# Two graph layers on one core: graphs singly in a pipeline, with x^T of layer 0 by DMA on 16-bit halves

## The chip, the cores and the metric

The kernel runs on one core of one Trainium2 chip. The metric is the device time of one execution in microseconds (us). The kernel before takes 3158.67 us, the median of three runs (3156.97 to 3158.88). The profiled execution spans 3156.3 us, with a mean granted TensorE clock of 0.996.

Engines are named as in the profile: PE is the matrix engine (PEld its weight loads), DVE the vector engine, ACT the scalar engine, POOL the general engine that also issues the accumulating DMAs, and SP the engine that issues plain DMAs. Each engine works through its own instructions in the order of the program and waits where a result of another engine is missing.

## What is computed

32 graphs of 512 nodes with 256 features, fp32 throughout. Each graph passes two layers with 8 heads of 32 features each; the layers have different masks, and only the first has a feed-forward part. Cut to what matters:

```python
# layer 0; allowed = (adj > 0) | (adj^T > 0) | eye
q, k, v = split(x @ Wqkv.T + bqkv)                     # 8 heads of 32
attn = softmax(where(allowed, q k^T / sqrt(32), -inf))
x1 = layernorm(x + (attn v) @ Wo.T + bo) * g1 + b1
ff = relu(x1 @ W1.T + b1) @ W2.T + b2                  # 256 -> 1024 -> 256
x2 = layernorm(x + layernorm(x1 + ff) * g2 + b2)
# layer 1; mask = adj != 0, other weights
out = layernorm(x2 + (softmax(mask(q k^T / sqrt(32))) v) @ Wo1.T + bo1)
```

The graphs do not depend on each other, so work of different graphs can be interleaved at will.

## The kernel before

A `Graph` object has one method for each step. The methods that matter here (p tiles are 128 x 2048 fp32, four heads by 512 queries, for one of the four blocks of 128 keys; k = 0 to 7 counts four key blocks for each of two head groups):

```python
def transpose(self, src, h):              # x^T on PE, half h of the nodes
    if h == 0:
        self.tile("xT", [ND, N], bufs=1)
    ps = ps_d.tile([P, ND, 2 * P], F32, tag="d", ...)
    for c in range(ND):
        for j in range(2):
            nc.tensor.transpose(ps[:, c, j*P:(j+1)*P], src[:, 2*h+j, c*P:(c+1)*P], ident)
    nc.scalar.copy(self.xT[:, :, h*2*P:(h+1)*2*P], ps)
...
def scores(self, layer, k):               # 4 heads at once, 32 rows of the array each
    s = ps_s.tile([P, HPC, N], F32, tag="s", ...)       # one buffer (bufs=1)
    for j in range(HPC):
        nc.tensor.matmul(s[:, j, :], self.kT[...], self.qT[...], start=True, stop=True)
    p = work.tile([P, HPC, N], F32, tag="p", ..., bufs=8)
    nc.scalar.activation(p, s, AF.Exp, scale=SCALE)
def masked(self, layer, k):
    nc.vector.tensor_tensor(p, p, m[:, k % NQ, None, :].to_broadcast(...), ALU.mult)
def product(self, k): ...                 # psA += v^T p, 4 heads; after kc 3 ACT copies it to cT
def pair(self, k):                        # p[k] += p[k+1] by an accumulating DMA from POOL
    nc.gpsimd.dma_start(out=self.p[k], in_=self.p[k + 1], accum_op=ALU.add)
def fold(self, dst, a, b):                # p[dst] = p[a] + p[b] on DVE
    nc.vector.tensor_tensor(self.p[dst], self.p[a], self.p[b], ALU.add)
def sums(self, k, hg, first, last):       # psR = ones^T p: the softmax sums
    if first:
        self.total = ps_d.tile([P, N], F32, tag="d", ...)
    ...
def divide(self, hg): ...                 # DVE: transpose, reciprocal, transpose, multiply cT
def out0(self, i): ...                    # DVE: residual sum and statistics (out1, out2 alike)
def root(self, n, a, b): ...              # POOL: (var + eps) ** -0.5
def norm1(self, i): ...                   # DVE (norm2, norm3 alike; norm4 on ACT)
def hidden(self, h, f): ...               # PE psH, then ACT relu into hT
def mlp(self, i): ...                     # PE psF
```

The interleaving is written out by hand in one list of calls. One period handles two graphs, c and d, together with the layer 1 that is left of graph b and the end of graph a:

```python
def period(a, b, c, d, e, f):
    b.scores(1, 0)
    b.masked(1, 0)
    ...                                   # (cut: layer 1 of b, layer 0 of c, layer 0 of d,
    ...                                   #  feed-forward of c and d, layer 1 of c)
    c.fold(3, 3, 4)
...
for k in range(-1, B // 2):
    period(*graphs[2 * k + 2 : 2 * k + 8])
```

After the loop one number, a sum of all softmax sums and reciprocals, is tested; a slower general form would run if it were out of range, which it isn't with these inputs.

Of the kernel before, what the change touches and what calls it, by code (L numbers as in the profile page):

```python
# [9 lines left out]
F32 = mybir.dt.float32  # L10
BF16 = mybir.dt.bfloat16
I32 = mybir.dt.int32
AF = mybir.ActivationFunctionType
# [13 lines left out]
def kernel(ctx: ExitStack, tc: tile.TileContext, t: dict, out: bass.AP):  # L27
# [121 lines left out]
    def plain(pools: ExitStack):  # L149
# [26 lines left out]
        class Graph:  # L176


            def __init__(self, b):
                self.b = b  # L180
                self.mv, self.rs, self.pf = {}, {}, {}
# [7 lines left out]
            def load(self):  # L189
                nc.sync.dma_start(out=self.tile("x", [NQ, D]), in_=x[self.b].rearrange("(c p) d -> p c d", p=P))  # L190

            def again(self):

                nc.sync.dma_start(out=self.tile("x1", [NQ, D]), in_=x[self.b].rearrange("(c p) d -> p c d", p=P))

            def cast(self):

                self.code = hbm.tile([N, N], BF16, tag="code", name=f"code_{self.b}")
                nc.gpsimd.dma_start(
                    out=self.code.rearrange("(p c) k -> p (c k)", p=P),  # L200
                    in_=adj[self.b].rearrange("(p c) k -> p (c k)", p=P),
                )

            def entries(self):

                nc.sync.dma_start(
                    out=self.tile("m0", [NQ, N], BF16), in_=self.code.rearrange("(c p) k -> p c k", p=P)
                )
                self.tile("m1", [NQ, N], BF16, bufs=4)
# [11 lines left out]
            def once(self):  # L221

                if self.b == 0:
                    value_bias(0)
                    graphs[3].masks()
# [10 lines left out]

            def transpose(self, src, h):

                if h == 0:
                    self.tile("xT", [ND, N], bufs=1)  # L240
# [8 lines left out]
            def value(self, layer, h):  # L249
                if h == 0:  # L250
                    self.tile("v", [NQ, D])
# [13 lines left out]
            def query_key(self, layer, which, c, h=None):  # L265

                tag = ("qT", "kT")[which]
                dst = getattr(self, tag) if c or h else self.tile(tag, [ND, N])
# [54 lines left out]

            def final(self):
# [3 lines left out]
            def sums(self, k, hg, first=False, last=False):  # L328

                if first:  # L330
                    self.total = ps_d.tile([P, N], F32, tag="d", name=f"psR_{self.b}_{hg}")
# [4 lines left out]
                for i in beats:  # L336
                    for j in range(HPC):
                        nc.tensor.matmul(  # L338
                            self.total[j * HD : (j + 1) * HD, :],
# [6 lines left out]
            def divide(self, hg):  # L346
# [3 lines left out]
                nc.vector.transpose(sT.rearrange("p a b -> p (a b)"), self.total)  # L350
# [125 lines left out]
        graphs = [Absent()] * 2 + [Graph(b) for b in range(B)] + [Absent()] * 4  # L476

        def period(a, b, c, d, e, f):

            b.scores(1, 0)
            b.masked(1, 0)
            b.query_key(1, 0, 1)
            b.scores(1, 2)
            b.query_key(1, 1, 1)
            b.scores(1, 1)
            b.masked(1, 2)
            a.sums(3, 1, first=True, last=True)
            a.divide(1)  # L490
            b.product(0)
            d.load()
            c.transpose(c.x, 0)
            b.scores(1, 3)
            c.transpose(c.x, 1)
            a.project(1, 0)
            b.masked(1, 1)
            a.out1(0)
            b.scores(1, 5)
            b.masked(1, 3)  # L500
            b.masked(1, 5)
            a.out1(1)
            d.again()
            b.product(1)
            b.pair(0)
            b.product(2)
            b.scores(1, 4)
            a.project(1, 1)
            b.pair(2)
            a.out1(2)  # L510
            c.query_key(0, 1, 0)
            b.masked(1, 4)
            b.scores(1, 7)
            a.out1(3)
            c.query_key(0, 0, 0)
            b.masked(1, 7)
            b.product(3)
            b.scores(1, 6)
            b.fold(2, 2, 0)
            b.product(4)  # L520
            b.residual2()
            a.root(4, 0, 2)
            b.pair(4)
            c.query_key(0, 1, 1)
            b.masked(1, 6)
            a.root(4, 2, 4)

            c.scores(0, 0)
            b.fold(3, 6, 7)
            c.query_key(0, 0, 1)  # L530
            a.offset(0, 2)
            b.sums(2, 0, first=True, last=True)
            a.norm4(1)
            b.divide(0)
            c.scores(0, 1)
            b.fold(3, 3, 4)
            b.product(5)
            b.product(6)
            c.masked(0, 1)
            c.masked(0, 0)  # L540
            c.once()
            b.product(7)
            c.scores(0, 7)
            c.value(0, 0)
            c.residual()
            b.sums(3, 1, first=True, last=True)
            a.norm4(0)
            b.divide(1)
            c.scores(0, 2)
            c.value(0, 1)  # L550
            d.transpose(d.x, 0)
            c.scores(0, 3)
            c.product(0)
            c.masked(0, 2)
            b.project(1, 0)
            c.scores(0, 6)
            c.masked(0, 3)
            c.product(1)
            b.out1(0)
            a.offset(2, 4)  # L560
            c.product(2)
            d.transpose(d.x, 1)
            c.scores(0, 4)
            c.masked(0, 7)
            b.out1(1)
            c.masked(0, 6)
            c.pair(0)
            a.norm4(3)
            d.query_key(0, 1, 0)
            c.pair(2)  # L570
            c.masked(0, 4)
            c.scores(0, 5)
            c.masked(0, 5)
            a.norm4(2)
            d.query_key(0, 0, 0)
            b.project(1, 1)
            c.fold(2, 2, 0)
            c.product(3)

            d.scores(0, 0)  # L580
            c.once1()
            c.fold(3, 6, 7)
            b.root(4, 0, 2)
            b.offset(0, 2)
            b.out1(2)
            a.store()
            b.out1(3)
            c.product(4)
            c.pair(4)
            c.product(5)  # L590
            c.sums(2, 0, first=True, last=True)
            d.masked(0, 0)
            c.product(6)
            d.scores(0, 1)
            c.divide(0)
            c.fold(3, 3, 4)
            b.norm4(0)
            d.value(0, 0)
            c.product(7)
            d.scores(0, 2)  # L600
            d.query_key(0, 0, 1)
            d.query_key(0, 1, 1)
            d.scores(0, 3)
            b.root(4, 2, 4)
            b.norm4(1)
            d.product(0)
            c.sums(3, 1, first=True, last=True)
            b.offset(2, 4)
            d.masked(0, 1)
            d.masked(0, 2)  # L610
            d.product(1)
            b.norm4(2)
            b.norm4(3)
            c.divide(1)
            d.residual()
            d.masked(0, 3)
            d.scores(0, 4)
            d.value(0, 1)
            d.scores(0, 6)
            c.project(0, 0)  # L620
            c.project(0, 1)
            c.out0(0)
            d.pair(0)
            d.scores(0, 7)
            d.product(2)
            c.out0(1)
            c.root(1, 0, 2)
            c.norm1(0)
            c.norm1(1)
            c.out0(2)  # L630
            d.pair(2)
            d.product(3)
            c.out0(3)
# [385 lines left out]
```

## Time and profile before

| | |
|---|---|
| Time, median of three runs | 3158.67 us |
| Span of the profiled execution | 3156.3 us |
| p masks on DVE (L295), 512 of 128x2048 | 1158.6 us, 2280 ns each |
| exponentials on ACT (L290), 512 of 128x2048 | 961.7 us, 1878 ns each |
| scores on PE (psS, L286) / products (psA, L303) | 584.8 / 510.4 us busy |
| feed-forward on PE (psH, L417 / psF, L438) | 460.1 / 454.3 us busy |
| transposes on PE (psT, L244), 768 of 128x128, three sets per graph | 127.9 us busy |
| copies of psT to xT on ACT (L247), 192 of 128x512 | 112.1 us, 584 ns each |

How to read it: "busy" of an engine is the union of its instructions' times, so groups that overlap add up to more than the engine's line. A group of instructions is named by the tile that it writes and the tiles that it reads. Idle time of an engine is put beside the releaser, the event that ended it. In views by stretch each line gives a stretch, its length, and then the busy time (and in brackets the instructions) of PE, PEld, DVE, ACT and POOL, the granted PE clock, the DMA share and the GB/s.

### The profile page before, as it was taken

To read this page: it belongs to the slowest core of one execution; us is meant where nothing else is said; L and a number is where in the kernel's file an instruction comes from. 1 tells how busy PE (TensorE), PEld (TensorE's weight loads), DVE (VectorE), ACT (ScalarE), POOL (GpSimd) and SP (SyncE) were. 2 spreads that over 40 slices of the span, in tenths; PEclk is the share of its full clock that TensorE was granted. 3 is DMA by queue.
4 is the path that set the end of the run, shared out by engine and by line. 5 is a ranking of instruction groups with operands and counts; after the bars stand their busy time and mean duration, and the time that the engine had idled before them with its cause. 6 is when DMAs were issued, how large, how long until landed. Compare 5 with 4: busy or idle time off the path is not lost.

```text
span 3156.3 us, 43843 instructions
## 1 busy us (share of the span) xinstructions
PE 3105.7 (98%) x17466; PEld 1751.6 (55%) x17466; DVE 2673.4 (85%) x3458; ACT 1683.5 (53%) x1921; POOL 895.4 (28%) x1254
## 2 busy tenths in 40 slices
PE   6999999999999999999999999999999999999998
PEld 2655637456474664746547465564655637456473
DVE  4889797897979879798897988979889798897977
ACT  4455464645646456464563645646455464554644
POOL 0232222332322323232232322322223222332322
PEclk8999999999999999999999999999999999999999
DMA  7656556664656647576465665656656556665633
GB/s 185 121 112 124 119 107 127 121 127 107 120 115 132 123 103 135 103 140 127 102 127 109 136 129 104 129 112 124 123 111 127 121 107 127 120 127 107 124 57 68
DMA packets 239876, 374.00 MB, mean 118 GB/s; under 512 B 80176, under 2 KB 214448, under 8 KB 214960
## 3 DMA queue, kind: packets, MB, share of 16 engines
q0 software_dynamic: 95824, 282.09, 49.2%
q1 hardware_dynamic: 143840, 89.03, 10.5%
q8 instruction: 139, 2.28, 0.3%
q14 instruction: 73, 0.60, 0.1%
HBM read 89.01 MB, written 33.55 MB: 39 GB/s over the span
## 4 chain that ended last, share of the span: by engine, by line
PE 89%; ACT 5%; DVE 3%; DMA 1%; SPq 1%; POOL 1%; issue 1%; POOLq 0%; DVEq 0%
PE psS L286 17%; PE psH L417 14%; PE psF L438 14%; PE psA L303 13%; PE psQK_None L273 8%; PE psV L256 6%; PE psO L397 6%; ACT p L290 5%; PE psR L338 4%; PE psQK L273 4%; PE psT L244 3%; DMA p<-p 1%; DVE st L366 1%; DVE x L381 1%; SPq L211 0%
## 5 line engine op out<-in xcount | busy, mean ns | idle before, releaser
L295 DVE TENSOR_TENSOR p<-p,m 128x2048 f32<-128x2048 f32 x512 | 1158.6, 2280 | 80.0 <-ACT p L290 78.2
L290 ACT ACTIVATE p<-psS 128x2048 f32<-128x2048 f32 x512 | 961.7, 1878 | 481.8 <-PE psS L286 379.8
L286 PE MATMUL psS<-qT,kT 32*128 32x512 f32 x4096 | 584.8, 641 | 11.1 <-ACT p L290 3.0
L303 PE MATMUL psA<-p,v 128*32 128x512 f32 x4096 | 510.4, 599 | 0.0
L417 PE MATMUL psH<-xT,w_L_gnn_W 128*128 128x256 f32 x2048 | 460.1, 381 | 0.0
L438 PE MATMUL psF<-w_L_gnn_W,hT 128*128 128x256 f32 x2048 | 454.3, 380 | 0.0
L322 DVE TENSOR_TENSOR p<-p,p 128x2048 f32<-128x2048 f32 x189 | 428.1, 2286 | 10.2 <-DMA p<-p 7.2
L417 PEld LDWEIGHTS psH<-xT,w_L_gnn_W 128*128 128x128 f32 x2048 | 383.9, 190 | 86.0 <-ACT xT L247 24.3
L438 PEld LDWEIGHTS psF<-w_L_gnn_W,hT 128*128 128x128 f32 x2048 | 384.1, 190 | 61.7 <-ACT hT L425 12.1
L372 POOL TENSOR_SCALAR rs<-mv 128x2 f32<-128x2 f32 (+1 forms) x320 | 190.8, 596 | 775.2 <-DVE mv L367 775.2
L425 ACT ACTIVATE hT<-psH,c_L_gnn_b 128x256 f32<-128x256 f32 x512 | 214.6, 470 | 285.9 <-PE psH L417 284.2
L286 PEld LDWEIGHTS psS<-qT,kT 32*128 32x128 f32 x4096 | 160.1, 183 | 312.3 <-issue 136.0
L318 POOL DMA_DIRECT2D p<-p x189 | 195.1, 1059 | 467.9 <-PE psA L303 295.0
L373 POOL TENSOR_TENSOR rs<-rs,neg_half 128x2 f32<-128x2 f32 (+1 forms) x320 | 286.1, 894 | 26.7
L303 PEld LDWEIGHTS psA<-p,v 128*32 128x32 f32 x4096 | 106.3, 109 | 314.9 <-issue 233.7
L273 PE MATMUL psQK_None<-xT,w_L_gnn_Wqkv 128*128 128x512 f32 x512 | 250.3, 618 | 4.7 <-DMA w_L_gnn_Wqkv<-in_L_gnn_Wqkv_dram 4.7
L397 PE MATMUL psO<-w_L_gnn_Wo,cT 128*128 128x256 f32 x1024 | 244.8, 384 | 0.7 <-DVE held L985 0.5
L397 PEld LDWEIGHTS psO<-w_L_gnn_Wo,cT 128*128 128x128 f32 x1024 | 187.9, 190 | 68.2 <-issue 40.6
L353 POOL TENSOR_TENSOR total<-total,sT 128x16 f32<-128x16 f32 x128 | 28.2, 221 | 654.1 <-DVE sT L350 645.1
L313 ACT COPY cT<-psA 128x512 f32<-128x512 f32 x128 | 74.9, 585 | 215.0 <-PE psA L303 206.7
L247 ACT COPY xT<-psT 128x512 f32<-128x512 f32 x192 | 112.1, 584 | 131.3 <-PE psT L244 131.1
L366 DVE BATCH_NORM_STATS2 st<-y 128x6 f32<-128x256 f32 x384 | 164.3, 428 | 13.1
(67 smaller groups left out, 2912.6 us busy)
## 6 DMA issues: line engine op xcount, KB each, us to landing
p<-p POOLq DMA_DIRECT2D x189, 1024.0 KB, 8.7
x<-in_x_dram SPq DMA_DIRECT2D x64, 512.0 KB, 5.3
x<-bov POOLq DMA_DIRECT2D x64, 512.0 KB, 5.8
code<-in_adj_dram POOLq DMA_DIRECT2D x32, 512.0 KB, 6.0
m<-code SPq DMA_DIRECT2D x32, 512.0 KB, 3.9
x<-s_L_gnn_ln_b POOLq DMA_DIRECT2D x32, 512.0 KB, 8.0
x<-s_L_gnn_b POOLq DMA_DIRECT2D x32, 512.0 KB, 6.0
out_dram<-x SPq DMA_DIRECT2D x32, 512.0 KB, 3.5
```

The costliest lines, as they stand in the source:

```text
L273: nc.tensor.matmul(ps, w[:, i, c * P : (c + 1) * P], self.xT[:, i, at], start=(i == 0), stop=(i == ND - 1))
L286: nc.tensor.matmul(s[:, j, :], self.kT[at, hg, kc * P : (kc + 1) * P], self.qT[at, hg, :], start=True, stop=True)
L290: nc.scalar.activation(p, s, AF.Exp, scale=SCALE)
L295: nc.vector.tensor_tensor(p, p, m[:, k % NQ, None, :].to_broadcast([P, HPC, N]), ALU.mult)
L303: nc.tensor.matmul(self.acc[hg][j * HD : (j + 1) * HD, :], self.v[:, kc, h * HD : (h + 1) * HD], self.p[k][:, j, :], start=(kc == 0), stop ...
L322: nc.vector.tensor_tensor(self.p[dst], self.p[a], self.p[b], ALU.add)
L366: nc.vector.bn_stats(st, y)
L373: nc.gpsimd.tensor_tensor(rs, rs, neg_half[:, a:b, None], ALU.pow)
L397: nc.tensor.matmul(ps[:, j, :], self.cT[:, k, at], wo[layer][:, k, :], start=(k == 0), stop=(k == ND - 1))
L417: nc.tensor.matmul(ps[:, j, :], w1[:, c, at], self.xT[:, c, h * 2 * P : (h + 1) * 2 * P], start=(c == 0), stop=(c == ND - 1),)
L425: nc.scalar.activation(self.hT[h][:, f + j, :], ps[:, j, :], AF.Relu, bias=b1[:, f + j : f + j + 1])
L438: nc.tensor.matmul(ps, self.hT[h][:, f, j * P : (j + 1) * P], w2[:, f, :], start=(f == 0), stop=(f == NF - 1))
```

## The change

The order is rebuilt around one graph. A period now handles layer 0 of graph c beside layer 1 of graph b, which is one graph ahead; a is what remains of layer 1 two graphs ahead, and d is prepared (x^T, q, k, v). The first half of the feed-forward part of a graph is in the period of its layer 0, the second half at the head of the next one. There are 35 periods in place of 17, each with half the work.

x^T of layer 0 no longer comes from PE (but for graph 0). A DMA transpose works on 16-bit elements, so x is read from memory as twice as many 16-bit halves, transposed, and then sorted by four DMAs per half of the nodes into low and high halves; ACT joins them to fp32 words with two strided 16-bit copies. The halves lie in v and kT, which are not yet in use then. The transposes of x1 and x2 stay on PE. The buffers of xT go from one to two, those of the layer-1 mask m1 from four to three. The sums of the two head groups have separate names, so that both can be alive.

```diff
+            def flip(self, n, i):
+                if i == 0:
+                    self.tile("v", [NQ, D])
+                    self.tile("kT", [ND, N])
...
+                elif self.b > 0:
+                    src = x[self.b, i * 2 * P : (i + 1) * 2 * P, :]
+                    nc.sync.dma_start_transpose(out=self.flipped(0, i), in_=src.bitcast(U16))
+            def sort(self, n, h):
...
+                for w in range(2):
+                    for i in range(2):
+                        nc.sync.dma_start(
+                            out=dst[i * P // 2 : (i + 1) * P // 2, w * ND : (w + 1) * ND, :], in_=src[w::2, i::2, :]
+                        )
+            def join(self, n, h):
+                if n == 0 and self.b == 0:
+                    self.transpose(self.x, h)
+                    return
...
+                for w in range(2):
+                    nc.scalar.copy(
+                        words[:, :, h * 2 * P : (h + 1) * 2 * P, w], self.sorted(n, h)[:, w * ND : (w + 1) * ND, :]
+                    )
-                    self.tile("xT", [ND, N], bufs=1)
+                    self.tile("xT", [ND, N])
-                self.tile("m1", [NQ, N], BF16, bufs=4)
+                self.tile("m1", [NQ, N], BF16, bufs=3)
-                    self.total = ps_d.tile([P, N], F32, tag="d", name=f"psR_{self.b}_{hg}")
+                    self.total[hg] = ps_d.tile([P, N], F32, tag="d", name=f"psR_{self.b}_{hg}")
```

The new list, cut to what the prediction speaks of (each call is one of the steps above):

```diff
-        def period(a, b, c, d, e, f):
+        def period(a, b, c, d, e):
+            c.scores(0, 0)
...                                        # b.hidden(1, 0 and 4)
+            a.fold(3, 6, 7)
...                                        # c.scores(0, 1), a.product(7), b.hidden(1, 6)
+            a.fold(3, 3, 4)
+            c.masked(0, 0)
+            c.scores(0, 3)
+            a.sums(3, 1, first=True, last=True)
+            c.product(0)
...                                        # hidden, scores, project and out1 of a, mlp(2), mlp(3), out2
+            b.norm2(2)
+            b.norm2(3)
+            b.root(3, 2, 3)
+            c.pair(2)
+            c.masked(0, 5)
+            c.product(5)
+            b.root(3, 3, 4)
+            b.norm3(2)
+            c.masked(0, 6)
+            b.norm3(3)
+            c.masked(0, 7)
+            a.offset(2, 4)
+            b.transpose(b.x2, 1)
+            c.pair(4)
...                                        # three query_key of b
+            c.fold(2, 2, 0)
+            b.scores(1, 0)
+            c.product(6)
+            c.sums(2, 0, first=True, last=True)
+            c.product(7)
+            c.fold(3, 6, 7)
+            c.fold(3, 3, 4)
+            b.scores(1, 1)
+            b.query_key(1, 0, 1)
+            c.sums(3, 1, first=True, last=True)
+            c.divide(0)
...                                        # scores of b, c.divide(1), project, out0, norm1 of c
+            d.flip(0, 0)
...                                        # d.again, d.load
+            d.sort(0, 0)
+            d.flip(0, 1)
+            a.store()
+            d.sort(0, 1)
+            c.transpose(c.x1, 0)
+            b.scores(1, 6)
+            c.hidden(0, 0)
+            d.join(0, 0)
...                                        # hidden of c, scores, products and masks of b
+            c.transpose(c.x1, 1)
+            d.join(0, 1)
...                                        # c.mlp(0), c.mlp(1), out2, norm2; value and query_key of d
+            b.scores(1, 7)
+            b.product(4)
+            b.fold(2, 2, 0)
+            c.norm3(0)
+            b.masked(1, 7)
+            c.norm3(1)
+            b.product(5)
+            b.product(6)
+            b.sums(2, 0, first=True, last=True)
+            b.divide(0)
...
+            for k in range(-1, B + 2):
+                period(*graphs[k + 1 : k + 6])
```

Before the first period the second graph's x is now loaded ahead of most of the weights.

## The prediction

> **What bounds the kernel now.** I read the page's busy shares and the chain of waits first, then busy time by stretches (two whole periods and both ends), then the order of PE and of DVE in single stretches.
>
> ```profile
> PE 3105.7 (98%) x17466; PEld 1751.6 (55%) x17466; DVE 2673.4 (85%) x3458; ACT 1683.5 (53%) x1921; POOL 895.4 (28%) x1254
> PE 89%; ACT 5%; DVE 3%; DMA 1%; SPq 1%; POOL 1%; issue 1%; POOLq 0%; DVEq 0%
> ```
>
> PE is busy for 98% of the span and is 89% of the chain. DVE, at 85%, is the next engine, and 15% is all the room it has. The stretches say where the 2% are:
>
> ```profile
> 0.00:20.00 20.00, 10.34 (x24) 5.12 (x28) 2.18 (x4) 3.99 (x6) 2.12 (x11) 1.00 0.89 218
> 20.00:40.00 20.00, 11.12 (x56) 5.21 (x52) 5.82 (x5) 9.89 (x8) 2.65 (x2) 0.86 0.98 245
> 40.00:60.00 20.00, 11.33 (x64) 3.88 (x68) 12.24 (x9) 7.27 (x6) 1.73 (x2) 0.71 0.80 174
> ...
> 450.00:644.00 194.00, 193.44 (x1091) 109.42 (x1090) 167.65 (x217) 105.40 (x122) 56.30 (x79) 1.00 0.61 120
> ...
> 3140.00:3160.00 20.00, 3.62 (x17) 2.69 (x16) 6.28 (x21) 3.27 (x6) 2.29 (x6) 0.81 0.17 57
> ```
>
> Between the ends PE idles 0.6 us in 194. A period repeats every 193.9 us (the stores of two periods start at 450.03 and 643.78, others at 526.73 and 720.69), so a graph costs 96.9 us. 16 periods are 3102 us; the remaining 54 us of the span are the ends, some 27 us of PE idle in the first 60 and 16 in the last 20. There is nothing to gain between the ends unless PE gets less to do.
>
> How PE's groups follow each other:
>
> ```profile
> 1255.77 0.96 PE L244 MATMUL psT<-ident,x 128*128 128x128 f32 x4
> 1256.65 1.14 PE L286 MATMUL psS<-qT,kT 32*128 32x512 f32 x8
> 1257.72 7.17 PE L417 MATMUL psH<-xT,w_L_gnn_W 128*128 128x256 f32 x32
> 1264.83 1.07 PE L303 MATMUL psA<-p,v 128*32 128x512 f32 x8
> 1265.82 0.66 PE L244 MATMUL psT<-ident,x 128*128 128x128 f32 x4
> 1266.32 7.07 PE L438 MATMUL psF<-w_L_gnn_W,hT 128*128 128x256 f32 x32
> 1273.23 7.07 PE L417 MATMUL psH<-xT,w_L_gnn_W 128*128 128x256 f32 x32
> ```
>
> From start to start, a psT group costs 0.5 us (1265.82 to 1266.32), seldom 0.9; scores 1.07; products 1.0 (less in a row); four hidden groups 7.1 after scores, but psF after psT 6.91: a wide group behind a narrow one (scores, products, sums) pays up to 0.19 us for a weight load that isn't hidden. Durations of single instructions overlap, so I use starts.
>
> And DVE where it is full:
>
> ```profile
> 1369.57 0.72 DVE L350 STREAM_TRANSPOSE sT<-psR 128x512 f32<-128x512 f32 x1
> 1370.32 0.25 DVE L352 RECIPROCAL r<-sT 128x16 f32<-128x16 f32 x1
> 1370.69 0.71 DVE L356 STREAM_TRANSPOSE rT<-r 128x512 f32<-128x512 f32 x1
> 1371.44 0.69 DVE L357 TENSOR_TENSOR cT<-cT,rT 128x512 f32<-128x512 f32 x1
> 1372.05 2.28 DVE L295 TENSOR_TENSOR p<-p,m 128x2048 f32<-128x2048 f32 x1
> 1374.37 0.42 DVE L385 TENSOR_TENSOR y<-psO,x 128x256 f32<-128x256 f32 x1
> ```
>
> divide is 2.45 us from start to start; in the same way a mask or a fold is 2.2, a residual with its statistics 1.0, norm2 1.5, norm1 1.05, norm3 0.35.
>
> **What the skill says.** The Trainium skill's "DMA: Bandwidth & Descriptors", section "Constraints" of the DMA transpose, has it take 2-byte elements only and write to SBUF, which is why x is split into halves. In this trace the transposes of the adjacency (512x128, bf16) land after 3.6 us in the median, at 1.26 us of SP's time each. "TensorE: Matmul & The Clock Gate", section "Architectural detail: the array is 16× 32×32, not 1× 128×128", calls the queues of ACT and DVE strict FIFO, with only PE's weight loads pulled ahead; the trace agrees, every engine starts its instructions in program order. So an operation that stands behind a late one is late too, and the written order decides. "ScalarE: Activation LUTs", section "What ACT_TABLE_LOAD costs", puts an ACTIVATE with immediate operands at 186 ns + 0.833 ns per element: 612 ns at 512 elements, where the copy of psT takes 584 here.
>
> **The change part by part.**
>
> 1. *Transposes off PE.* Two psT groups per graph go, 2 x 0.5 = 1.0 us, rarely more, for 31 of 32 graphs (graph 0 keeps PE): -31 to -34 us, all of it on the path, as PE is full.
>
> 2. *Fewer changes from narrow to wide.* In program order two graphs have 30 such changes before and 26 after, so 2 fewer per graph: 2 x 0.19 = 0.38 us, -12 us. With 1 this makes 96.9 - 1.45 = 95.45 us per graph, -45 us in all.
>
> 3. *DMA, SP, ACT.* Per graph two flips (131072 halves each, twice an adjacency transpose, estimated at 2.5 us of SP and 4 to 6 us to landing) and eight sorts (0.4 to 0.5 us to issue, 3.5 to 4 to land, from like transfers). The first flip waits for v of the layer 0 just done, at about 47 us into the period; flip, sort, flip, sort end at about 65; the second join stands on ACT at about 75. That is 10 us of slack, so I count nothing. ACT gets four copies of 512 elements (estimated 0.6 us each) for two: +1.2 us in a graph where it has 43 us idle.
>
> 4. *The ends.* Before, the first period has two layer-0 graphs to mix, and still loses 27 us. After, graph 0 is alone in its period. Its PE work, with q, k, v of graph 0 and 1, is some 61 us; chaining its steps (first scores at 21, masks at 2.2 each, the accumulating DMAs at 8.7, divide, project, norm1, hidden, mlp) I get to graph 1's scores at about 93 us, 32 us idle. At the end graph 31 has half its feed-forward and layer 1 alone: about 24 us idle beside 18 before, and the period ahead of it has no d. Against that, the second x loads earlier (before, PE sat 15.6 us for it). Sum: +6 us, 0 to +20.
>
> 5. *Waits in the new period.* I laid PE's groups end to end by the costs above, and DVE's beside them. Time 0 is c.scores(0, 0). The last scores of b end 3.7 us before it, exp takes 1.88, so b's last mask ends at 0.5. Then norm3 and divide to 3.4, two folds to 7.8, c's first mask to 10: its product on PE is due at 10.7. The residuals of a wait for its project (16.9), and DVE goes on without a gap to 29.7 (out2(3)). norm2(3) waits for root on POOL (32.0), ends at 33.5; the mask of 5 ends at 35.7, of 6 at 38.3; norm3(3) at 38.7. PE wants to transpose x2 at 37.4: it waits 1.3 us. pair(2) is issued at about 33.7, behind root(3, 2, 3), and lands at 42.4 with the 8.7 us of the page; fold(2, 2, 0) ends at 44.6, and the sums on PE, due at 44, wait 0.7. scores(1, 3) has 1.92 us of other work in front for 1.88 of exp: 0.2. Further on every operation is ahead of its user. So up to 2.2 us a period, where before it was 0.3 per graph. The two large ones hang on durations right at the limit, and the list looks tuned (norm1(1) ahead of norm1(0), hidden 0, 2, 6, 4), so I take a third: 0.7 x 31 = +22 us.
>
> Sum: 3158.7 - 45 + 6 + 22 = 3141.7, rounded down to 3140 us, since the small waits of before (0.3 per graph) are in part replaced and not kept.
>
> **The rivals.**
>
> *The order holds, no new wait.* Then PE stays at 99.5% between the ends: 3158.7 - 45 + 0 to 6 = 3114 to 3120. For it: DVE's mean load would be 83.5 of 95.5 us (2673.4 / 32), and the half of the period with the feed-forward part has DVE in hand. Against it: the first half of the period.
>
> *DVE sets the period's first half.* From 0 to 50 us DVE has about 47 us of work in my layout, with five hand-overs to POOL, PE and DMA in it. If all 2.2 us come, and pair lands nearer to the 14.7 us that is its longest here, the period is 97.5 to 99 us: 3158.7 - 45 + 6 + 31 x (2 to 3.6) = 3182 to 3231. Against it: before, too, DVE runs gaplessly for 50 us in each period and PE doesn't stop.
>
> *The DMA of x^T is late.* DMA engines are busy 61% in a period, and the accumulates (1 MB each) come in bursts. Flips and sorts that land 10 us later than I think would make ACT wait at the join, and behind it the exponentials, for a few us each period: 3200 and more. For it: eleven dependent issues of SP in one queue, with a.store amid them. Against it: the 10 us, and that the hardware queue now takes 9.7% of the DMA engines in a period, of which the adjacency's transposes are only a part.
>
> **Range and chances.** Best case 3105 to 3120, with my full waits about 3187. I give 3100 to 3195 eight in ten. Faster by over 2% (below 3095.5) would need ends shorter than before as well: 0.07. Slower by over 2% (above 3221.8) needs rival two or three in full: 0.10. Within 2%: 0.83.
>
> **What the profile would show.** Step 1: psT from 768 to about 520 instructions, 3 us less of PE in 194. Step 2: stores in steady state 95.5 us apart plus the waits. Step 3: no idle of ACT put down to a DMA at the join. Step 4: PE busy in the first 100 us some 62 us, and 25 us idle in the last 60. Step 5: idle of PE or PEld before psT of x2, released by DVE's norm3 (L454 before), and before psR, released by a fold or the DMA of p. The prediction is wrong if the distance of stores falls outside 95.2 to 97.7 us, if DVE waits for the pairs by more than 1 us in each period, or if the ends lose over 25 us more than before.

## The result, and the profile after

The changed kernel takes 3192.31 us, the median of four runs (3190.82 to 3199.04), against 3158.3 us for the kernel before in the same session: 1.0112 times as long, 95% interval 1.0095 to 1.013. The forecast was a fall of 18 us; the time rose by 34.

The page of the changed kernel, busy time by engine:

```profile
PE 3085.0 (97%) x17218; PEld 1737.2 (54%) x17218; DVE 2665.0 (84%) x3458; ACT 1724.2 (54%) x1983; POOL 1131.3 (35%) x1254
```

PE has 20.7 us less to do than in the kernel before, where 45 were forecast, and the span grew all the same: PE now stands still for 106 us of 3191, before for 51 of 3156. Busy time by stretches shows where; columns as before (the first is the stretch, PE comes after the length, and the granted clock is third from the end):

```profile
0.00:20.00 20.00, 10.75 (x31) 7.57 (x32) 2.87 (x5) 4.32 (x6) 2.09 (x11) 1.00 0.79 211
20.00:40.00 20.00, 13.88 (x60) 3.99 (x59) 6.30 (x4) 9.75 (x8) 0.92 (x1) 0.83 1.02 263
40.00:60.00 20.00, 15.29 (x92) 3.89 (x90) 16.89 (x9) 7.92 (x5) 4.35 (x4) 0.76 1.06 217
60.00:80.00 20.00, 13.10 (x50) 8.29 (x43) 14.17 (x28) 1.25 (x3) 4.01 (x9) 0.73 0.89 164
80.00:100.00 20.00, 20.00 (x87) 15.72 (x86) 8.56 (x21) 8.56 (x17) 3.48 (x6) 1.00 0.25 32
...
1068.60:1165.40 96.80, 95.35 (x540) 53.93 (x536) 83.38 (x109) 53.58 (x62) 35.90 (x39) 1.00 0.70 131
...
3100.00:3120.00 20.00, 15.69 (x70) 9.93 (x71) 15.56 (x18) 4.43 (x10) 4.82 (x7) 0.83 0.26 53
3120.00:3140.00 20.00, 16.28 (x71) 13.28 (x74) 9.43 (x30) 3.78 (x8) 7.11 (x13) 0.91 0.11 18
3140.00:3160.00 20.00, 15.74 (x80) 5.42 (x76) 10.85 (x5) 14.51 (x12) 0.00 (x0) 0.91 0.15 37
3160.00:3180.00 20.00, 18.03 (x137) 5.72 (x138) 12.08 (x14) 4.93 (x4) 0.88 (x4) 0.92 0.00 1
```

The line in the middle is one quiet period: 95.35 us of PE work per graph. Two graphs took 193.25 of 193.80 us in a like stretch of the kernel before:

```profile
1000.00:1193.80 193.80, 193.25 (x1096) 109.21 (x1088) 167.28 (x216) 105.17 (x121) 55.97 (x78) 1.00 0.62 120
```

So the work per graph fell by 1.27 us, while the idle time rose from 0.28 to 1.45. The other lines are the ends. From 20 to 80 us and from 3100 to 3180 us PE is between two thirds and nine tenths busy, at a granted clock of 0.73 to 0.92. The thin stretches of the kernel before, shown in the prediction, are shorter and emptier: 60 us at the start with 10.3 to 11.3 of 20 us busy, and the last 16.

The view of waits names what PE stood for between 1000 and 2000 us (total us, times, longest us). Of the kernel before this view has no line at all for PE in that stretch:

```profile
PE psT L298 <- DVE x L513: 9.4, 11, 1.1
PE psT L298 <- DVE x L440: 5.5, 10, 0.6
PE psR L397 <- DVE p L376: 1.3, 3, 0.7
PE psA L357 <- ACT p L344: 1.2, 1, 1.2
```

The first is the transpose of x2, which waits for norm3, the second the transpose of x1, which waits for norm1: once each in nearly every period. The last two are sums and products that wait in single periods.

### The profile page after: what moved, and what is told of

Read it like the earlier page. It is cut to its first block, busy times and chain, and to the rows that moved or that the text cites. A ratio compares the mean times of both kernels' runs of the same rounds, so it can differ in the third digit from the quotient of the medians.

```text
span 3191.1 us, 44297 instructions
## 1 busy us (share of the span) xinstructions
PE 3085.0 (97%) x17218; PEld 1737.2 (54%) x17218; DVE 2665.0 (84%) x3458; ACT 1724.2 (54%) x1983; POOL 1131.3 (35%) x1254
## 5 line engine op out<-in xcount | busy, mean ns | idle before, releaser
L431 POOL TENSOR_SCALAR rs<-mv 128x2 f32<-128x2 f32 (+1 forms) x320 | 374.2, 1169 | 784.1 <-DVE mv L426 783.1
L357 PE MATMUL psA<-p,v 128*32 128x512 f32 x4096 | 501.2, 602 | 4.4 <-ACT p L344 3.5
L476 PE MATMUL psH<-xT,w_L_gnn_W 128*128 128x256 f32 x2048 | 477.8, 386 | 0.7 <-ACT xT L301 0.7
L376 DVE TENSOR_TENSOR p<-p,p 128x2048 f32<-128x2048 f32 x189 | 429.3, 2285 | 47.8 <-DMA p<-p 44.9
L476 PEld LDWEIGHTS psH<-xT,w_L_gnn_W 128*128 128x128 f32 x2048 | 379.7, 190 | 149.9 <-issue 77.9
L432 POOL TENSOR_TENSOR rs<-rs,neg_half 128x2 f32<-128x2 f32 (+1 forms) x320 | 347.5, 1086 | 26.7
L456 PE MATMUL psO<-w_L_gnn_Wo,cT 128*128 128x256 f32 x1024 | 252.3, 390 | 3.2 <-DVE cT L416 2.7
L327 PE MATMUL psQK_None<-xT,w_L_gnn_Wqkv 128*128 128x512 f32 x512 | 230.9, 594 | 0.0
L330 ACT ACTIVATE kT<-psQK_None,c_L_gnn_bqkv 128x512 f32<-128x512 f32 x64 | 44.0, 687 | 285.2 <-PE psQK_None L327 285.2
L397 PE MATMUL psR<-p,ones 128*32 128x512 f32 x1072 | 142.0, 606 | 15.5 <-DVE p L376 14.8
## 6 DMA issues: line engine op xcount, KB each, us to landing
x<-in_x_dram SPq DMA_DIRECT2D x64, 512.0 KB, 11.5
```

The lines of the kernel that those rows point to most:

```text
L327: nc.tensor.matmul(ps, w[:, i, c * P : (c + 1) * P], self.xT[:, i, at], start=(i == 0), stop=(i == ND - 1))
L357: nc.tensor.matmul(self.acc[hg][j * HD : (j + 1) * HD, :], self.v[:, kc, h * HD : (h + 1) * HD], self.p[k][:, j, :], start=(kc == 0), stop ...
L431: nc.gpsimd.tensor_scalar(rs, self.mv[n][:, a:b, 1:2], EPS, None, ALU.add)
L432: nc.gpsimd.tensor_tensor(rs, rs, neg_half[:, a:b, None], ALU.pow)
L456: nc.tensor.matmul(ps[:, j, :], self.cT[:, k, at], wo[layer][:, k, :], start=(k == 0), stop=(k == ND - 1))
L476: nc.tensor.matmul(ps[:, j, :], w1[:, c, at], self.xT[:, c, h * 2 * P : (h + 1) * 2 * P], start=(c == 0), stop=(c == ND - 1),)
```

## Experiments

**A. The ends, or every graph?** Both kernels were run with the first 16 graphs only (B = 16 in the loop; the rest of the output is left out). The difference between 32 and 16 graphs gives the cost of a graph, and what is left is that of the ends.

> The changed kernel with only graphs 0 to 15 (the other 16 outputs are not computed). Theory 1 (most of the loss is at the ends): in the changed kernel's trace a graph costs 97.2 us and what is left is 81 us, so 81 + 16 x 97.2 = 1636 us, 31 above the kernel before with 16 graphs. Rival (the loss is spread over all periods): the difference to before halves, 34 / 2 = 17 us, so about 1622 us.

> The kernel before with only graphs 0 to 15. Both theories: 54.6 us of ends and 16 x 96.93, so 1605.5 us; it is the measure for the run of the changed kernel with 16 graphs.

Measured: 1638.66 us for the changed kernel, 1606.91 for the one before; 31.75 apart, nearly as much as with 32 graphs.

| | per graph | ends |
|---|---|---|
| before | (3158.26 - 1606.91) / 16 = 96.96 | 3158.26 - 32 x 96.96 = 55.6 |
| after | (3192.31 - 1638.66) / 16 = 97.10 | 3192.31 - 32 x 97.10 = 85.0 |

The ends cost 29.4 us more. In steady state 0.14 us per graph is lost, 4.6 us in all, where 0.7 was to be gained. The split is known to a few us: with the fastest and the slowest of the four runs of the changed kernel the ends cost 31 and 23 us more. That most of the loss is there stands in either case.

**B. x^T of layer 0 back on PE, in the new order.** flip and sort do nothing, join transposes on PE:

```diff
-                if n == 0 and self.b == 0:
+                if n == 0:
                     self.transpose(self.x, h)
                     return
```

> The changed order, but x^T of layer 0 by PE for all graphs, as before. Theory 1 (the DMA transposes do what they are for): two psT groups come back, 31 x 1.0 = +31 us, 3223 us. Rival (the DMA of x^T crowds the accumulating DMAs, whose lateness costs what PE saves): the waits shrink as the transposes come back, and the time stays at 3185 to 3200 us.

Measured 3246.85 us (1.0283 times before, interval 1.0266 to 1.0301), 54.5 more than the changed kernel, 1.76 per graph, and outside both ranges. PE's busy time rises by 31.2 us, from 3085.0 to 3116.2, which is the 1.0 per graph that the transposes were to cost. The rest is waiting: between 1000 and 2000 us PE's waits rise from 17.4 to 27.1 us, all of it at the sums (11.8 in place of 1.3). Without the flips in SP's queue the x loads go out earlier, beside c's pairs (1016.36 and 1020.00 us, pairs at 1020.36 and 1024.12). That this makes the sums late is my reading of the trace; no run tests it alone.

```profile
1038.18 1.06 PE L399 MATMUL psR<-p,ones 128*32 128x512 f32 x8 [1.73 <-DVE p L378]
```

So the DMA path is worth its trouble in this order. It is the order that gives the gain away: with the same transposes on PE it is 88.6 us slower than the order before.

**C. norm3(3) ahead of the mask of block 6,** to take the largest wait of a period away:

```diff
             b.norm3(2)
-            c.masked(0, 6)
             b.norm3(3)
+            c.masked(0, 6)
```

> The changed kernel with b.norm3(3) ahead of c.masked(0, 6) on DVE, nothing else. Theory 1 (PE waits for norm3 at the transpose of x2, 1.0 us a period, only because a mask stands in front of it): -1.0 x 31, 3161 us. Rival (DVE has no room in this half of the period): the wait moves to the sums behind fold(2, 2, 0), and the time is 3185 us or more.

Measured 3193.96 us (1.0119, 1.0102 to 1.0135): nothing gained. PE's waits from 1000 to 2000 us now:

```profile
PE psR L397 <- DVE p L376: 10.1, 14, 1.0
PE psT L298 <- DVE x L440: 5.5, 10, 0.6
```

The 9.4 us at the transpose of x2 are gone, and 8.8 more stand at the sums of layer 0.

**D. Residual adds moved.** POOL issues these accumulating DMAs close behind the pairs; moved away, they should let the pairs land earlier for DVE's folds: c.residual up behind c.once, b.residual2 down before e.cast; then the same with C.

> The changed kernel with the three accumulating DMAs of the residuals moved on POOL: c.residual up to just behind c.once, b.residual2 down to just ahead of e.cast; nothing else. Theory 1 (the pairs of p land late because the residuals are issued on their heels): DVE's wait for the DMA of p, 1.5 us a period, shrinks; PE's wait for the sums is only 0.1 us a period, so the time falls by 0 to 0.5 us a graph, 3177 to 3192 us. Rival (the pairs are late because they are issued late): no change in DVE's wait.

> The same with b.norm3(3) ahead of c.masked(0, 6) as well. Theory 1 (DVE has room for norm3 in front once the pairs land earlier): PE's wait at the transpose of x2 goes and doesn't come back at the sums, -1.0 x 31, 3161 us. Rival (this half of the period is DVE's own work from end to end): 3185 us or more, with the wait at the sums.

Measured 3203.74 us (1.0151, 1.0134 to 1.0168) and 3212.04 (1.0182, 1.0155 to 1.021). The first lies above its range of 3177 to 3192. Both lose mostly at the start: the first sums of graph 1 stand at 149.9 and 155.5 us, in the changed kernel at 140.5, which is 9.4 of the 11.4 us lost and 15.0 of the 19.7. In quiet periods of the second the folds wait for no pair, and PE still waits 0.79 us at the sums.

**E. DVE work left out.** First one fold between the two sums of layer 0 (C's kernel without c.fold(3, 6, 7); row sums are incomplete):

> The kernel of the run with b.norm3(3) ahead of c.masked(0, 6), and c.fold(3, 6, 7) of layer 0 left out (one 128x2048 add of 2.3 us on VectorE per graph; the output lacks part of the row sums, so only the time is read). Theory, VectorE's own work sets the first half of a period: TensorE's waits at the sums of layer 0 go and the distance of two graphs falls by 0.8 to 1.3 us (97.1 to about 96.0), the time to 3155 to 3170. Rival, the wait at the sums is one for the transfer of the pair or for the latency of product to sum: the distance stays at 97.1 and the time at 3185 to 3196.

Measured 3195.71 us (1.0128, 1.0112 to 1.0145). The fold behind it then waits for the pair instead, here in a line of DVE's timeline:

```profile
1020.80 2.29 DVE L376 TENSOR_TENSOR p<-p,p 128x2048 f32<-128x2048 f32 x1 [2.56 <-DMA p<-p]
```

So neither DVE's load nor the pairs alone is the limit. The next three kernels let the pair land and the fold come earlier (C's kernel, with):

```diff
             b.norm2(2)
+            c.pair(2)
             b.norm2(3)
             b.root(3, 2, 3)
-            c.pair(2)
...
             c.masked(0, 6)
+            c.fold(2, 2, 0)
             c.masked(0, 7)
...
-            c.fold(2, 2, 0)
```

The first of them also has b.masked(1, 1) behind c.norm1(0), so that norm1 comes earlier:

> The changed kernel in an order meant to take TensorE's three short waits of a period away at once: b.norm3(3) ahead of c.masked(0, 6), c.pair(2) issued ahead of b.root(3, 2, 3) and so about 2 us earlier, c.fold(2, 2, 0) ahead of c.masked(0, 7) on VectorE, and b.masked(1, 1) behind c.norm1(0). Theory, the steady part is held up only by these waits, each the end of a chain on VectorE or a pair's landing that the order places: the quiet distance of 96.8 falls by 0.8 to 1.3 and the time to 3150 to 3172. Rival, VectorE or the transfers refill whatever is freed, as in the runs before: 3185 to 3196.

Measured 3255.61 us (1.0309, 1.0292 to 1.0327), far above both ranges. The wait at the transpose of x1 went, but the product that uses the moved mask paid for it, 1.87 us in each period. With the mask back at its place:

> The run with the early fold, with b.masked(1, 1) back at its place ahead of c.root(1, 0, 2), from where its move cost TensorE 1.87 us of waiting per period at b.product(1). Theory, VectorE's own work in front of the sums of layer 0 is the limit: TensorE still waits 0.8 to 1.2 us there per period (for a mask, a fold or both) and the time is 3180 to 3196. Rival, the order alone was the limit: 3155 to 3172.

Measured 3199.35 us (1.0133, 1.0116 to 1.015), 3 us above the range of the theory, with waits of the kind that it named; quiet periods are 97.1. PE's waits from 1000 to 2000 us:

```profile
PE psR L397 <- DVE p L376: 8.3, 12, 1.0
PE psA L357 <- DVE p L349: 5.9, 11, 1.1
PE psT L298 <- DVE x L440: 5.4, 10, 0.6
```

Then the same without c.masked(0, 6), a DVE instruction in front of both folds (that block stays unmasked):

> The same with c.masked(0, 6) of layer 0 left out (one 128x2048 multiply of 2.3 us on VectorE per graph, in front of both folds; scores of one block of keys stay unmasked in the output, so only the time is read). Theory: with 2.3 us less in front of the sums TensorE's wait there goes and the time falls by 20 to 40 us against the run with this mask, to 3145 to 3172. Rival, the landing of the pairs takes over at once: within 8 us of it.

Measured 3200.16 us (1.0133, 1.0116 to 1.0149), one single period of 105.9 among them; quiet ones are 96.9 in place of 97.1. Between 1000 and 2000 us DVE's waits for pairs rise from 4.7 to 27.0 us:

```profile
DVE p L376 <- DMA p<-p: 27.0, 15, 3.6
```

The 2.3 us of DVE work came back almost whole as a wait for the pair. Last, PE's own part moved back by about 1 us (c.product(7) behind b.scores(1, 1), c.sums(3, 1) behind b.scores(1, 2)):

> The run with the early pair, with c.product(7) behind b.scores(1, 1) and c.sums(3, 1) behind b.scores(1, 2), so that TensorE comes to both some 1 us later. Rival, order: the two waits of 0.43 and 0.67 us per period go, and the time falls by 20 to 34 us to 3165 to 3180. Theory, from the pair over folds, sums, divide and norm1 to the second transpose runs one chain without slack, near the length that TensorE gives it: the waits reappear behind it (at the projection or at the transpose of x1), the period stays within 0.4 us of 97.1 and the time at 3185 to 3205.

Measured 3199.74 us (1.0144, 1.0123 to 1.0165), and quiet periods of 97.1 again:

```profile
PE psT L298 <- DVE x L440: 9.8, 10, 1.0
PE psO L456 <- DVE cT L416: 4.9, 10, 0.5
PE psR L397 <- DVE p L376: 1.7, 4, 0.7
```

Both waits left the sums and the product, and stand at the projection and at the transpose of x1 instead. PE's waits in these 1000 us add up to 17.4 us after the change (the four lines shown), 16.8 in C with one of 1.2 not shown, 20.8 with the early pair, 17.8 here (the last two with waits of 1.2 and of 1.4 not shown). The waits change their places, and their sum stays between 16.8 and 20.8 us.

**F. The ends filled.** At the start graph 1's x^T (by PE), q, k and v go between the first scores of graph 0; at the end the second half of graph 31's feed-forward part is pulled up into its own period. First with norm2 and norm3 pulled up too, then with these behind the sums and the divide of graph 30:

```diff
+            if k == 0:                    # amid c.scores(0, 2) to c.product(5)
+                d.join(0, 0); d.join(0, 1); d.value(0, 0) ...
+            if k == B - 1:                # from c.mlp(1) on
+                c.hidden(1, 0) ... c.mlp(2); c.mlp(3); c.out2(2); c.out2(3) ...
```

> The changed kernel with other ends, the periods between them untouched: in the period of graph 0 alone, x^T (by PE), q, k and v of graph 1 are put between the scores of graph 0, where PE waits for exponentials; in the last period with layer 0, the second half of the feed-forward part of graph 31 is pulled up to where the q, k and v of a next graph would be. Theory 1 (29 us of the 34 are PE idle at the ends): about -10 at the start and -15 to -20 at the end, 3162 to 3167 us. Rival (the ends are latency chains that don't shorten by moving PE work): 3185 us or more.

> As the run with both ends filled, but of graph 31 only the second half of the feed-forward goes up into period 31; its norm2 and norm3 of the last two rows, their roots and the second transpose come behind the sums and the divide of graph 30. Theory (the end lost there because these norms stood ahead of graph 30's folds on VectorE and held ScalarE's queue): the time from graph 31's layer-0 sums to its last sums falls from 120.1 to 105 to 112 us and, with 7 us kept at the start, the time is 3175 to 3187. Rival (the end is a chain of one graph's layer 1, whatever is pulled up): 118 us or more, 3188 to 3196.

Measured 3194.41 us (1.0116, 1.0099 to 1.0132) and 3195.18 (1.0119, 1.0103 to 1.0136). The start gains 7 to 8 us in both (first sums of graph 1 at 133.3 and 132.6 us), and the end loses as much: from graph 31's first sums to its last ones it takes 120.1 and 118.4 us, where the changed kernel takes 111.4. PE at the end of the first and of the second:

```profile
3122.49 1.94 PE L397 MATMUL psR<-p,ones 128*32 128x512 f32 x8 [9.76 <-DVE p L376]
```

```profile
3120.70 1.93 PE L397 MATMUL psR<-p,ones 128*32 128x512 f32 x8 [6.43 <-DVE p L376]
3128.93 0.45 PE L298 MATMUL psT<-ident,x 128*128 128x128 f32 x1 [6.30 <-DVE x L513]
```

Work that is pulled up fills period 31 and puts the sums of graph 30 later; behind them PE has nothing left to put into the waits. The fill of the start alone, on the kernel with the early fold and the moved mask:

> The same with the fill of the start alone (graph 1's x^T by TensorE and its q, k, v between the first scores of graph 0), and nothing pulled up at the end. Theory, the 7 us that the two runs with both ends filled gained at the start are kept where the end is left as it was: 5 to 8 us under the run without the fill. Rival, the start's gain is lost later: within 2 us of it.

Measured 3250.6 us (1.0299, 1.0282 to 1.0316), 5.0 under the 3255.61 of the same without the fill: at the start a part can be won back, as far as four runs each can tell (3252.99 to 3262.07 and 3249.03 to 3254.19).

**G. x^T by DMA in the order of before.** The same transposes, staged in the buffer of hT, which is free between two feed-forward parts: for both graphs of a period, for the first (c) or the second (d) alone.

```diff
+            def flip(self):
+                if self.b < 2:                       # or: also self.b % 2 == 1, == 0
+                    return
+                t = work.tile([P, NF, 2 * P], F32, tag="hT", ..., bufs=1)
...
-            c.transpose(c.x, 0)
+            c.join(0)
...
-            c.transpose(c.x, 1)
+            c.join(1)
+            d.flip()
+            d.sort()
...                                        # d.join for d.transpose; behind d.mlp(3):
+            e.flip()
+            e.sort()
```

> The two-graph order of before with one part of the change alone: x^T of layer 0 by DMA on 16-bit halves for graphs 2 to 31, staged in the buffer of hT while that is free. Theory 1 (the transposes off PE are worth their PE time, in a full order that has room for them): 2 psT groups x 0.5 us x 30 graphs, 3158 - 30 = 3128 us; up to 1.27 us a graph, the fall of PE's busy time per graph in the changed kernel, 3120 us. Rival (the DMA chain of flip and sort is late or crowds the accumulating DMAs): PE waits at the queries, 3158 us or more.

> The order of the kernel before with x^T by DMA for the first graph of each pair only (graphs 2, 4 ... 30; flips and sorts behind d.mlp(3)). Theory, the loss of the run with both comes from the flips and sorts of the second graph, which are issued while the pairs of b are in flight: no fold waits over 2 us for a pair, and TensorE's saving of about 1 us per graph shows: 3140 to 3158. Rival, every flip costs the same wherever it stands: half of the loss of 90 us, 3195 to 3210.

> The same for the second graph of each pair only (graphs 3, 5 ... 31; flips and sorts right behind c.join, beside the pairs of b). Theory: the whole loss stands here, folds wait some 80 us in all for pairs and the time is 3230 to 3260. Rival: half of it, 3195 to 3210.

| x^T by DMA for | time, us | ratio to before, interval | folds wait for pairs |
|---|---|---|---|
| both | 3248.18 (3231.41 to 3287.49) | 1.0288 (1.0238 to 1.0338) | 91.3 us, longest 17.0 |
| c only | 3152.47 | 0.9984 (0.9977 to 0.9991) | 11.5 us, longest 1.5 |
| d only | 3155.32 | 0.9996 (0.9987 to 1.0005) | 7.5 us, longest 1.1 |

Of the four runs of both, the one of 3287.49 us had a lower granted clock (0.980, in the profiled run 0.987) and is left out of the ratio; the other three took 3231.41 to 3261.90. Each alone costs nothing, which I had not expected of d. Nor does it gain much: c alone takes 10.0 us of busy time off PE (3095.7 against 3105.7), 0.67 us for each of its 15 graphs where 1.0 was expected, and half of that shows in the time. The queue of SP in one period of d alone shows why (start, us, ...):

```profile
1155.16 5.18 SPq L246 DMA_TRANSPOSE stage<-in_x_dram  x2
1160.70 8.83 SPq L255 DMA_DIRECT2D stage<-stage  x8
```

b's pairs of that period are issued at 1178.77, 1182.09 and 1192.47. With c's x^T in the same buffer, d's flips have to wait for c's join and come some 23 us later, beside the pairs. To tell the place from the number, d alone was run with its flips held back by a tiny copy of ACT into the staging buffer, behind ACT's copy of c's x^T:

> The kernel before with x^T by DMA for the second graph of each pair only, and its flips held back until ScalarE has copied the second half of the first graph's x^T (a copy of 128x2 into the staging buffer, which the flips then wait for), so that they start where they started in the run with both. Without the hold they were issued some 24 us earlier and had landed before b's pairs. Theory, where a flip stands decides, beside the pairs or not: folds wait 50 us or more in all for pairs, 3215 to 3255. Rival, it takes the flips of both graphs, their number: folds wait under 20 us, 3150 to 3165.

Measured 3200.45 us (1.0133, 1.0099 to 1.0166), 45 more than without the hold. The same queue, where the pairs go out at 1203.26, 1206.58 and 1216.96, and DVE's wait over the whole run:

```profile
1202.94 3.63 SPq L247 DMA_TRANSPOSE stage<-in_x_dram  x2
1209.82 11.82 SPq L256 DMA_DIRECT2D stage<-stage  x8
```

```profile
DVE p L358 <- DMA p<-p: 60.5, 22, 19.0
```

The wait is as the theory had it, the time below its range. It is uneven: two folds of the run waited 19.0 and 10.1 us, the others 3.0 at most. PE's waits for the sums and for the scores are 33.0 and 16.4 us in all, 2.9 and 1.9 with d alone, and that makes up the 45. So the same flips are harmless in one place and cost 45 us in another. In the changed kernel, too, a pair goes out beside the second flip (at 1033.42 and 1033.55 us), but the next fold on DVE starts at 1060.55, and no pair of the whole run took over 12.0 us to land. DVE's waits for pairs are 44.9 us in all, and 55.3 without the flips (B), so the place chosen there is harmless. The kernel with c alone is also the only one of all these runs that beats the kernel before, by 0.16%: the fastest kernel of this study is the old order with half of the new transposes.

## Why the prediction was wrong

The time was to be 3141.7 us before rounding and was 3192.3, so 50.6 us were missed. By the runs of A the ends make 23 of them (29.4 us in place of 6), the waits in the period 23 (45 in place of 22), and the saving on PE 4 (41 in place of 45). Two steps failed, to about equal parts.

*Steps 1 and 2, PE's work.* Right in kind, near in size. psT fell from 768 to 520 instructions; PE's work per graph fell by 1.27 us in the place of 1.45. B puts 1.0 of that on the transposes; what is left for the second step is 0.27 in place of 0.38.

*Step 3, DMA, SP, ACT.* My costs were too low: a flip lands after 10.4 us (4 to 6 expected), a joining copy takes 0.78 us (0.6), as the lists of DMA issues and of groups by form show:

```profile
v<-in_x_dram SPq DMA_TRANSPOSE x62, 10.4
kT<-v SPq DMA_DIRECT2D x248, 64.0 KB, 4.1
```

```profile
L286 ACT COPY xT<-kT 128x512 uint16<-128x512 uint16 x124 | 88.0, 775 | 12.0 <-DMA kT<-v 11.8
```

ACT waited 11.8 us for sorts in the whole run, and no wait of PE is put down to it: "I count nothing" held. That rival is out in this order, and G shows what it would have cost elsewhere.

*Step 4, the ends: its sum failed.* "+6 us, 0 to +20" was +29.4 by the runs of A, outside its own range; by the distances (97.21 us between sums, see below, and 96.94 before) it is 26. The forecast had graph 1's first scores at 93 us behind 61 us of PE work; they came at 102.7 us, behind 75.7, of which a mean clock of 0.87 accounts for 13 at most. For the first 100 us it had 62, and the profile shows 73.0 (the first five lines of stretches above). Idle time is not what was missed: in the first 140 us it is 27.2 (before 27.4), from 3040 us to the end 25.8 (before 14.4). The earlier load of the second x did what was said of it, PE's wait for x fell from 20.5 to 4.5 us, and waits inside graph 0 took its place. What the sum lacked is that PE's work itself takes longer where PE is not kept busy. The same eight matmuls of the sums, in a full period and at the end:

```profile
1015.52 1.04 PE L397 MATMUL psR<-p,ones 128*32 128x512 f32 x8
3103.57 1.93 PE L397 MATMUL psR<-p,ones 128*32 128x512 f32 x8 [4.15 <-DVE p L376]
```

The granted clock falls short of 1.00 by 23.9 us summed over the stretches of the ends, and by 11.7 before (each stretch times one minus its clock; an upper estimate, as it counts idle time as well). With 11 more of idle time these 12 make about 23 of the 29 us; the rest I can't place, and no run here held the clock fixed. The Trainium skill says so of the chip in "TensorE: Matmul & The Clock Gate", section "What's actually happening": by default the array's clock is throttled, and activity releases it. The trace agrees, with 1.00 in full stretches and 0.73 to 0.92 in those shown above, but for the first 20 us, which had 1.00 with PE 54% busy. My reading, not tested by itself, is that one graph at a time has long, thin ends, where two in mixture filled their own waits.

*Step 5, waits in the period: the mechanism right, the size wrong.* Both large waits of the list are there, the transpose of x2 behind norm3 with 0.83 us (1.3 expected) and the sums behind the fold (0.7 expected), which the first one hides in most periods and C uncovered. One was not in the list, the transpose of x1. It is the second line here, behind that of x2 in the same period:

```profile
1010.42 0.55 PE L298 MATMUL psT<-ident,x 128*128 128x128 f32 x3 [0.83 <-DVE x L513]
1034.49 0.66 PE L298 MATMUL psT<-ident,x 128*128 128x128 f32 x4 [0.55 <-DVE x L440]
```

In front of it, norm1 waits 0.63 us for a root on POOL, which runs beside a mask of DVE. In the timelines of POOL and DVE:

```profile
1029.80 2.17 POOL L431 TENSOR_SCALAR rs<-mv 128x2 f32<-128x2 f32 x1 [4.70 <-DVE mv L426]
1056.71 0.35 POOL L431 TENSOR_SCALAR rs<-mv 128x2 f32<-128x2 f32 x1 [7.31 <-DVE mv L426]
```

```profile
1029.62 2.26 DVE L349 TENSOR_TENSOR p<-p,m 128x2048 f32<-128x2048 f32 x1
1032.91 0.48 DVE L440 SCALAR_TENSOR_TENSOR x<-cent,rs,s_L_gnn_ln_b 128x256 f32<-128x256 f32 x1 [0.63 <-POOL rs L432]
```

The same operation takes 0.35 to 0.51 us beside a 0.45 us step of DVE and 0.22 where DVE stands still (at 99.39 us). In the first line it ends 0.1 us after the mask. "SBUF — State Buffer", section "Who interferes with whom", has it that a DVE instruction with two SBUF inputs contends with a GpSimd (POOL) instruction that reads SBUF; the lines fit that. The mean of this line on the page is 1169 ns, in the kernel before 596, so the new order puts more roots beside masks and folds. With the mask moved behind norm1 (the first kernel with the early fold in E) the wait at this transpose went; whether the mask's own place on DVE or the slowed root made it, no run tells apart.

By the runs of A the waits take 0.14 + 1.27 = 1.41 us per graph, 45 us in all, two thirds of the 2.2 that the layout gave, and I had taken one third. (The view of waits, 17.4 us in 1000, gives 1.7.) So the 41 us of PE's work that were saved went into waits, and the ends came on top. "The two large ones hang on durations right at the limit" was true, but not a reason to discount them: E shows a chain without slack, from the last masks over pair, folds, sums, divide, projection and norm1 to the transpose of x1. Whatever is relieved in it shows up further down.

*The rivals.* "The order holds" is out. "DVE sets the period's first half" was nearest, with a time that its range of 3182 to 3231 holds; but E takes the reason apart. 2.3 us less of DVE's work in front of the folds gave 0.2 us per period, since the fold then waits for the pair's landing. It is DVE and the pairs in one chain. Not tried: an order that gives this chain more than one graph's distance.

*The signs named.* The distance of sums in steady state, 97.21 us on average (96.8 in quiet periods, 98.5 in the longest), lies within 95.2 to 97.7, and DVE's wait for the pairs, 44.9 us in all, was over 1 us in 19 of 32 periods, not in each. The third sign, ends that lose over 25 us more, came, though only just if the ends are taken from the distances, with 26.

## What to carry to other kernels

Work taken off a full engine pays only if the chain that feeds it is shorter than the new period; lay that chain out end to end, and count each wait that the layout shows in full. An order with fewer independent pieces in flight can pay at both ends, and here the busy engine's work took longer there as well, so run a shorter problem to part the ends from the steady state. A background transfer is placed against the transfers that others soon wait for: the same one was free at one place and cost 45 us when issued 23 us later.

## What the runs showed of the hardware

- DMA transposes and their sorts beside accumulating DMAs held these up: 1 MB pairs took up to 26.0 us to land with the flips of both graphs and 28.0 with those of one in the wrong place, 14.7 in the kernel before, and a fold waited up to 17.0 and 19.0 us for one, 1.3 before.
- A POOL operation on two numbers per partition took 2.17 us beside a 2.26 us DVE multiply of two SBUF operands, 0.35 to 0.51 beside a 0.45 us step, and 0.22 while DVE stood still.
- PE's granted clock averaged 0.73 to 0.92 over 20-us stretches that were 66 to 90% busy, and 0.59 in one of 63% (12.54 of 20 us, at the end of the first kernel of F). The first 20 us, 54% busy, had 1.00.
